# Graph attention loop: value products interleaved bank by bank and two steps behind, densities in halves at pinned places, the entry check at the end of the step

## The chip, the cores and the metric

The kernel runs on one core of one Trainium2 chip. A core has five engines, each with its own in-order instruction queue: TensorE (PE, matrix products into PSUM banks), VectorE (DVE), ScalarE (ACT, functions such as exp and ln), GpSimd (POOL, here mostly the issuer of gathers) and SyncE (SP, issuer of plain transfers). ACT can issue transfers as well. The engines order themselves against each other by semaphores only. The metric is the device time of one execution in microseconds. Before the change the median of three runs is 846.97 us (839.39 to 852.38).

## The reference

A graph of 2708 nodes with 128 features and a 0/1 adjacency matrix `adj` goes through four layers, each `x = x + layer(relu(layernorm(x)))`: an attention layer, a normalised convolution, a convolution with batch norm, and a dense attention layer. The change lies in the last one, but for one line in its preparation:

```python
XW = h @ W
s_col = XW @ a[0, :f]
s_row = XW @ a[0, f:]
Z1 = leaky_relu(s_row[:, None] + s_col[None, :], negative_slope=0.01)
den = exp(Z1)
num = A @ den
att = where(num != 0, den / where(num != 0, num, 1.0), 0.0)
H = A @ (att @ XW)
```

So there are two products with A around a division, and the one in the middle, `att @ XW`, runs over all pairs of nodes.

## The kernel before

`binary` computes everything for a 0/1 matrix and counts entries that are neither 0 nor 1. A `general` path behind it is only entered when that count is above zero.

**Preparation of the last layer (L538 to L1074).** Since `exp(leaky(r + c))` is `exp(r) exp(c)` on one side of a kink and `exp(0.01 r) exp(0.01 c)` on the other, nodes are ranked by their row score, cut into 22 chunks of 124, and columns are grouped by the chunk in which their kink lies. `ranks` (L667) finds the ranks. For each tile t of 128 nodes VectorE compares a row of scores with the tile's own scores (the tile `bits`, t x 128 wide), TensorE adds up its columns (L687), and its row sums go into `rowsum`. For even t VectorE makes the row sums itself, in the same instruction (L680). For odd t VectorE only compares (L674), and ScalarE runs over `bits` again with an accumulating pass (L676). All of `rowsum` is needed for `below` (L789), from which the ranks, the tables of indices and everything after follow. Prefix sums of adjacency rows go to DRAM (`pre_d`, L1070 to L1073).

**The attention loop (L1169 to L1208).** It has NE = 22 steps. Each step covers 128 columns of `den` against all 2708 nodes, in two half steps q = 2s and 2s + 1. What a step needs and makes:

- *Rows.* For each half step a gather `g` fetches 124 rows of the transposed adjacency as 8-bit numbers (`fetch`, L1127), a gather `r` fetches 4 rows of prefix sums straight into the last rows of the moving operand (`fetch_pre`, L1130), and VectorE widens `g` into the first 124 (`widen`, L1138 to L1141). Once a step, a gather `xw` fetches the 128 value rows (`fetch_xw`). All five go through GpSimd (L1079). `g` has 4 buffers, `r` has 4, `xw` has 4.
- *Densities.* `densities` (L1095 to L1121) makes the stationary operands for four half steps at once, every second step: eight exponentials on ScalarE (`z` L1113, `lower` L1114), and on VectorE a maximum (L1115), a rounding (`d_hi`, L1118) and the remainder (`d_lo`, L1119), all 512 wide. The column scores come from a transfer on SyncE (`c_row`, L1110), for the first eight half steps (FIRST = 8) from a TensorE product with `diag` (L1100, L1107). `z` and `lower` have two buffers.
- *Sums.* For each of six banks of up to 512 nodes, four matmuls (L1180: two half steps, high and low part) add up `num` in one of two PSUM buffers, and ScalarE takes its logarithm from there (`ln`, L1182).
- *Weights.* ScalarE takes exp(-ln) over the whole 2708 (L1191) and VectorE multiplies with the numerator into `e` (L1193).
- *Value products.* TensorE adds `xw` times `e` to six accumulator banks. `spread_values(s - 1)` (L1146 to L1152) issues the six products of the step before in one block, after the six banks of sums of this step.
- *Check.* In every even step ScalarE's queue issues a load of one tile of the transposed adjacency (1354 KB, L1206), and in the step after VectorE checks it (`check`, L425 to L429, a pass over 2708 columns).

**What sets the order.** Instructions under `tc.keep_in_program_order` keep their order among each other on their engine. All others are placed by the framework's planner. Pinned are the sum and value matmuls, `ln`, the exponential L1191, `e`, `widen` and the loads for the check. The density work of ScalarE and VectorE, the check itself and the gathers are not pinned. On VectorE the recorded order of a pair of steps in the middle of the loop is: `r`, `r` (widen), `chk`, `r`, `r`, `e`, `d_hi`, `d_lo`, `z`, `e`. In that order the check stands ahead of the widening of a step.

**After the loop.** The last step's weights are made in six pieces, the value products of step 21 are added (L1281) and turned (`values`, L1235), and the last product with A (L401) begins. Its moving operand comes from 8-bit tiles `a8`: group 0 is loaded into the buffer that the checks used (`slot`, one buffer, loaded by ScalarE's queue, L1218), groups 1 to 5 by SyncE (L1229). VectorE and ScalarE widen them (L394, L392).

## Time and profile before

The profiled execution took 844.06 us, of which the trace covers 841.9 us (the span). Busy times in it:

| engine | busy us | share of the span | instructions |
|---|---|---|---|
| PE | 687.0 | 82% | 2700 |
| DVE | 578.8 | 69% | 1063 |
| ACT | 440.7 | 52% | 633 |
| POOL | 261.5 | 31% | 187 |

Places in the span (us from its start), by the timeline:

| from | to | what |
|---|---|---|
| 388 | 430 | ranks of the last layer |
| 493.87 | 754.07 | sums of the attention loop, first matmul of step 0 to last of step 21 |
| 754.07 | 768.83 | value products of steps 20 and 21; wait for the first tiles of the last product |
| 768.83 | 841.9 | last product with A, output |

The loop's steps can be told apart by the start of the wide exponential L1191, one per step (the last step's in pieces): 502.90, 516.40, 527.98, 537.77, 556.06, 566.74, 581.18, 592.96, 605.66, 616.86, 633.35, 644.33, 654.23, 664.10, 673.97, 688.85, 698.83, 709.29, 719.17, 735.13, 745.00, 754.72.

How to read a line of the timeline: start, duration, engine, line of the kernel, operation, output <- inputs with their shapes, the number of instructions merged into the line, and in brackets the idle time before it with what ended that idle time. A line of a group has the count, then busy time and mean ns of one, then the idle time ahead of the group's instructions.

### The profile page before, as it was taken

The page shows a single profiled execution, that of the slowest core. Times are in us where ns is not written, and L with a number is a line of the kernel's source. Part 1 is how long each engine was busy: PE and PEld are TensorE (multiplying, and loading weights), DVE is VectorE, ACT ScalarE, POOL GpSimd, SP SyncE. Part 2 cuts the span into 40 slices and gives each one's busy share as a digit, 9 for nine tenths or more (in the row PEclk, how much of TensorE's full clock was granted, in tenths as well). Part 3 has the DMA queues.
Part 4 walks back from the last instruction along what each step waited for, and adds up shares of the span by engine and source line. Part 5 has one row for each costly group of instructions (what it writes and reads, how often), then busy time and mean ns, then how long its engine had stood idle before and what let it go on. Part 6 is the DMA issues. An engine that isn't in the chain of part 4 may idle for free.

```text
span 841.9 us, 8176 instructions
## 1 busy us (share of the span) xinstructions
PE 687.0 (82%) x2700; PEld 420.6 (50%) x2700; DVE 578.8 (69%) x1063; ACT 440.7 (52%) x633; POOL 261.5 (31%) x187
## 2 busy tenths in 40 slices
PE   3899999918778789968759746978879989897995
PEld 2443343316556557644337334545546656464884
DVE  4886879577976666558999568556668756765433
ACT  3646766550662565348720387664645646462552
POOL 3101112220000010012002266756786888820000
PEclk9999999967999899988979869988999999898998
DMA  9189999801998154201001355654344445418002
GB/s 335 38 319 411 424 402 382 318 18 65 394 408 307 51 182 157 67 7 39 31 1 28 96 134 137 156 123 132 93 106 135 133 127 155 131 50 315 1 13 57
DMA packets 46521, 136.30 MB, mean 162 GB/s; under 512 B 13041, under 2 KB 24803, under 8 KB 38939
## 3 DMA queue, kind: packets, MB, share of 16 engines
q1 hardware_dynamic: 28341, 93.85, 30.6%
q0 software_dynamic: 15840, 25.82, 10.8%
q10 hardware_dynamic: 2289, 16.02, 6.3%
q8 instruction: 23, 0.38, 0.2%
q14 instruction: 28, 0.22, 0.1%
HBM read 116.84 MB, written 18.77 MB: 161 GB/s over the span
## 4 chain that ended last, share of the span: by engine, by line
PE 24%; DVE 12%; DMA 9%; issue 4%; ACT 4%; POOL 2%; DVEq 0%; POOLq 0%; ACTq 0%
PE acc L401 7%; PE bank L1180 7%; PE acc L1149 6%; DMA g<-adjt_d,row_i 4%; DMA chk<-in_adj_t_dram 4%; DVE r L1140 2%; DVE bits L680 2%; PE acc L825 1%; DMA a<-adjt_d 1%; DVE e L1193 1%; ACT ln L1182 1%; POOL r L1079 1%; ACT z L1113 1%; ACT lower L1114 1%; DVE own L659 1%
## 5 line engine op out<-in xcount | busy, mean ns | idle before, releaser
L1180 PE MATMUL bank<-r,d_hi 128*128 128x512 f32 (+1 forms) x264 | 109.6, 419 | 39.7 <-ACT ln L1182 24.2
L1182 ACT ACTIVATE ln<-bank,tiny 128x512 f32<-128x512 f32 x132 | 81.8, 634 | 86.0 <-PE bank L1180 83.0
L1149 PE MATMUL acc<-e,xw 128*128 128x512 f32 x252 | 107.3, 578 | 3.6 <-DVE e L1193 3.6
L1079 POOL DMA_INDIRECT g<-adjt_d,row_i x44 | 89.0, 2022 | 46.9 <-DVE row_i L1006 29.4
L1180 PE MATMUL bank<-r,d_lo 128*128 128x512 f32 (+1 forms) x264 | 101.9, 395 | 0.0
L280 PE MATMUL acc<-tau,hw 128*128 128x512 f32 (+1 forms) x240 | 97.2, 551 | 2.6 <-DVE tau L291 2.1
L392 ACT CAST m<-a 128x2048 fp32r<-128x2048 fp8e4 (+1 forms) x44 | 58.2, 1322 | 65.9 <-PE acc L401 57.8
L1193 DVE SCALAR_TENSOR_TENSOR e<-row_b,sig,ln 128x2708 f32<-128x2708 f32 (+2 forms) x27 | 67.3, 2511 | 34.4 <-ACT ln L1191 34.4
L394 DVE CAST m<-a 128x2048 fp32r<-128x2048 fp8e4 (+2 forms) x59 | 56.1, 954 | 47.0 <-PE acc L401 28.5
L1180 PEld LDWEIGHTS bank<-r,d_hi 128*128 128x128 f32 x264 | 53.3, 202 | 69.2 <-ACT ln L1182 44.2
L291 DVE SCALAR_TENSOR_TENSOR tau<-row_b,sg,a 128x1536 f32<-128x1536 f32 (+1 forms) x44 | 70.4, 1627 | 24.2 <-DMA a<-in_adj_dram 16.3
L1079 POOL DMA_INDIRECT r<-pre_d,pre_i x44 | 74.7, 1698 | 26.5 <-PE bank L1180 11.0
L1140 DVE CAST r<-g 124x2708 fp32r<-124x2708 fp8e4 x44 | 69.3, 1609 | 17.7 <-DMA g<-adjt_d,row_i 11.8
L1149 PEld LDWEIGHTS acc<-e,xw 128*128 128x128 f32 x252 | 49.4, 203 | 58.7 <-issue 54.7
L155 POOL TENSOR_TENSOR rstd<-isq,neg_half 128x4 f32<-128x4 f32 (+1 forms) x24 | 23.3, 972 | 169.2 <-DVE isq L154 155.9
L401 PE MATMUL acc<-m,y_hi 128*128 128x512 f32 (+1 forms) x132 | 54.1, 413 | 25.3 <-DVE m L394 22.6
L309 ACT ACTIVATE a<-a 128x2708 fp8e4<-128x2708 f32 x22 | 54.1, 2457 | 39.2 <-issue 22.4
L280 PEld LDWEIGHTS acc<-tau,hw 128*128 128x128 f32 x240 | 42.5, 190 | 61.5 <-issue 50.5
L401 PE MATMUL acc<-m,h_hi 128*128 128x512 f32 (+1 forms) x132 | 53.0, 406 | 7.4 <-ACT m L392 6.6
L1180 PEld LDWEIGHTS bank<-r,d_lo 128*128 128x128 f32 x264 | 53.7, 203 | 7.2
L1079 POOL DMA_INDIRECT xw<-xw_d,xw_i x22 | 44.5, 2020 | 34.4 <-PE acc L1149 18.0
L1191 ACT ACTIVATE ln<-ln 128x2708 f32<-128x2708 f32 (+2 forms) x27 | 54.6, 2041 | 0.6
(437 smaller groups left out, 1265.0 us busy)
## 6 DMA issues: line engine op xcount, KB each, us to landing
a<-in_adj_t_dram SPq DMA_DIRECT2D x25, 1354.0 KB
a<-in_adj_dram SPq DMA_DIRECT2D x21, 1354.0 KB
chk<-in_adj_t_dram ACTq DMA_DIRECT2D x10, 1354.0 KB
adj_d<-a POOLq DMA_DIRECT2D x22, 338.5 KB
adjt_d<-adjt SPq DMA_DIRECT2D x5, 1354.0 KB
a<-adjt_d SPq DMA_DIRECT2D x4, 1354.0 KB
a<-adj_d SPq DMA_DIRECT2D x5, 1024.0 KB
c_row<-ctwo_d SPq DMA_DIRECT2D x9, 256.0 KB
```

Of the source, the lines that this page charges most:

```text
L280: nc.tensor.matmul(accs[b][:, : hi - lo], stationary, tau[b // 3][:, o : o + hi - lo], start=first, stop=last)
L291: nc.vector.scalar_tensor_tensor(tau, row_b[:, h0:h1], sg[:, t : t + 1], a[:, h0:h1], ALU.max, ALU.mult)
L392: nc.scalar.copy(m[:, : hi - lo], src[:, lo:hi])
L394: nc.vector.tensor_copy(m[:, : hi - lo], src[:, lo:hi])
L401: nc.tensor.matmul(accs[b][:, : hi - lo], part[:, t, :], m[:, lo - base : hi - base], start=first and i == 0, stop=last and i == 1,)
L1079: return nc.gpsimd.indirect_dma_start(out=out, out_offset=None, in_=src, in_offset=bass.IndirectOffsetOnAxis(ap=idx, axis=0),)
L1140: ins = nc.vector.tensor_copy(rows_r[q][:CH], g[:CH])
L1149: m = nc.tensor.matmul(ys_acc[b][:, : hi - lo], xws[s], e[:, lo:hi], start=(s == 0), stop=(s == NE - 1))
L1180: m = nc.tensor.matmul(num[:, : hi - lo], d, a[:, lo:hi], start=(i == 0), stop=(i == 3))
L1182: tc.keep_in_program_order(nc.scalar.activation(ln[:, lo:hi], num[:, : hi - lo], AF.Ln, bias=tiny))
L1191: tc.keep_in_program_order(nc.scalar.activation(ln[:, lo:hi], ln[:, lo:hi], AF.Exp, scale=-1.0))
L1193: nc.vector.scalar_tensor_tensor(e[:, lo:hi], row_b[:, lo:hi], sig[:, s : s + 1], ln[:, lo:hi], ALU.max, ALU.mult)
```

## The change

The sums, products, gathers and checks stay the same in number and size. These things are different:

- **Value products.** Step s issues the value products of step s - 2, and bank by bank: four sum matmuls of bank b, then the value product of bank b. Those of step 20 come after the loop, those of step 21 where they were. `e` gets 3 buffers (2 before), `xw` gets 5 (4).
- **Densities.** Each step makes those of two half steps, for the step two later. The four exponentials are pinned, two after the logarithm of bank 1 and two after that of bank 2. The three VectorE instructions are 256 wide and are issued before the step's two widenings. `z` and `lower` get 3 buffers of half the width. `c_row` comes in 20 transfers half as wide, fetched two steps ahead. The first densities are four half steps (FIRST = 4), after the first two widenings instead of before.
- **Check.** It is pinned at its place in the program: the end of the step after the load, behind `e`. In the last step this is behind the last piece of `e`.
- **Ranks.** ScalarE makes the row sums of all tiles with t > 5 (of odd t before), VectorE those of t = 1 to 5 (of even t before).

In the recorded order of the changed kernel, VectorE's instructions of a step are: `z`, `d_hi`, `d_lo`, `r`, `r`, `e`, and after every second step `chk`. ScalarE's are: `ln`, `ln`, `z`, `lower`, `ln`, `z`, `lower`, `ln`, `ln`, `ln`, and the wide exponential.

```diff
-            if t % 2:
+            if t > 5:
                 ts_(bits[:r, : t * P], row_b[:r, : t * P], r_of[:r, t : t + 1], None, ALU.is_gt)
...
-    FIRST = 8
+    FIRST = 4
...
+    def exponents(s, p, z, lower, q):
+        nc_s = nc.scalar.activation
+        tc.keep_in_program_order(
+            nc_s(z[:, q, :], p[:, cols(q)], AF.Exp, bias=r_hi[:, s : s + 1], scale=slope_hi)
+        )
+        tc.keep_in_program_order(
+            nc_s(lower[:, q, :], p[:, cols(q)], AF.Exp, bias=r_lo[:, s : s + 1], scale=slope_lo)
+        )
+
+    def density_tiles():
+        z = steps.tile([P, 2, P], F32, tag="z", name="z", bufs=3)
+        lower = steps.tile([P, 2, P], F32, tag="lower", name="lower", bufs=3)
+        return z, lower
+
+    def densities(s0, z, lower):
         nc.vector.tensor_max(z, z, lower)
-        d_hi = steps.tile([P, 4, P], F32R, tag="d_hi", name="d_hi", bufs=4)
-        d_lo = steps.tile([P, 4, P], F32R, tag="d_lo", name="d_lo", bufs=4)
+        d_hi = steps.tile([P, 2, P], F32R, tag="d_hi", name="d_hi", bufs=4)
+        d_lo = steps.tile([P, 2, P], F32R, tag="d_lo", name="d_lo", bufs=4)
         nc.vector.tensor_copy(d_hi, z)
         nc.vector.tensor_sub(d_lo, z, d_hi.bitcast(F32))
...
+    def fetch_c(s0):
+        c_rows[s0] = p = steps.tile([P, 2 * P], F32, tag="c_row", name="c_row", bufs=4)
+        nc.sync.dma_start(p, ctwo_d[s0 * P : (s0 + 2) * P].partition_broadcast(P))
...
-        w = xws[s] = last.tile([P, P], F32, tag="xw", name="xw", bufs=4)
+        w = xws[s] = last.tile([P, P], F32, tag="xw", name="xw", bufs=5)
...
-    def spread_values(s):
-        e = waiting.pop(s)
-        for b, (lo, hi) in enumerate(E0):
...
+    def spread_value(s, b):
+        lo, hi = E0[b]
+        m = nc.tensor.matmul(
+            ys_acc[b][:, : hi - lo], xws[s], waiting[s][:, lo:hi], start=(s == 0), stop=(s == NE - 1)
+        )
+        tc.keep_in_program_order(m)
...
-        if s % 2 == 0 and FIRST + 2 * s < NS:
-            densities(FIRST + 2 * s)
+        coming = FIRST + 2 * s
+        if coming + 4 < NS:
+            fetch_c(coming + 4)
+        if coming < NS:
+            z, lower = density_tiles()
...
             tc.keep_in_program_order(nc.scalar.activation(ln[:, lo:hi], num[:, : hi - lo], AF.Ln, bias=tiny))
+            if coming < NS and 1 <= b <= 2:
+                exponents(coming + b - 1, c_rows[coming], z, lower, b - 1)
+            if s > 1:
+                spread_value(s - 2, b)
+        if coming < NS:
+            densities(coming, z, lower)
...
-        e = last.tile([P, N], F32, tag="e", name="e", bufs=2)
+        e = last.tile([P, N], F32, tag="e", name="e", bufs=3)
...
-        if s:
-            spread_values(s - 1)
         if pending:
-            check(*pending.pop())
+            tc.keep_in_program_order(check(*pending.pop()))
...
+    for b in range(NB):
+        spread_value(NE - 2, b)
```

## The prediction

> **What bounds the kernel now.** I read the chain of waits first. Inside the attention loop it runs over the landing of the check's tile, VectorE, ScalarE's exponentials and the sums, so the loop is not simply full of matmuls. Then I dated the steps by the wide exponential. From step 11 to 14 they are 9.9, 9.87 and 9.87 us apart. This is TensorE's own pace: in the chain of waits such a step is 5.28 us of sums and 4.59 us of value products. Steps 0 to 11 take 141.4 us against 11 x 9.87 = 108.6, so 32.9 are lost. Steps 14 to 19 take 61.2 against 49.4, so 11.8 are lost. The two losses have different causes.
>
> The first, in the timeline of one slow step:
>
> ```profile
> 541.47 2.98 DVE L427 SCALAR_TENSOR_TENSOR chk<-chk 128x2708 f32<-128x2708 f32 x1 [4.99 <-DMA chk<-in_adj_t_dram]
> ...
> 544.37 3.05 DVE L1140 CAST r<-g 124x2708 fp32r<-124x2708 fp8e4 x2
> ...
> 547.34 3.02 DVE L1193 SCALAR_TENSOR_TENSOR e<-row_b,sig,ln 128x2708 f32<-128x2708 f32 x1
> ...
> 550.74 0.69 DVE L1119 TENSOR_TENSOR d_lo<-z,d_hi 128x512 fp32r<-128x512 f32 x1
> 551.46 0.49 ACT L1113 ACTIVATE z<-c_row,r_hi,slope_hi 128x128 f32<-128x128 f32 x1 [7.13 <-DVE d_lo L1119]
> ...
> 552.58 0.79 PE L1180 MATMUL bank<-r,d_hi 128*128 128x512 f32 x1 [7.00 <-ACT ln L1182]
> ```
>
> VectorE stands at the check until its tile has landed. The remainder `d_lo` comes four instructions later, ScalarE needs it to reuse `z`, the logarithms are queued behind that exponential, and TensorE lacks a bank.
>
> The second, by GpSimd's groups in the two parts of the loop (494 to 643, then 643 to 742):
>
> ```profile
> L1079 POOL DMA_INDIRECT g<-adjt_d,row_i x24 | 46.1, 1919 | 11.7 <-issue 6.1 <-DVE r L1140 4.7 <-DVE d_lo L1119 0.6
> L1079 POOL DMA_INDIRECT r<-pre_d,pre_i x22 | 31.4, 1428 | 15.3 <-PE bank L1180 10.4 <-issue 4.6 <-PE acc L1149 0.3
> L1079 POOL DMA_INDIRECT xw<-xw_d,xw_i x10 | 25.6, 2558 | 19.2 <-PE acc L1149 18.0 <-issue 1.2
> ```
>
> ```profile
> L1079 POOL DMA_INDIRECT g<-adjt_d,row_i x16 | 38.0, 2377 | 4.9 <-issue 4.9
> L1079 POOL DMA_INDIRECT r<-pre_d,pre_i x18 | 37.6, 2088 | 5.5 <-issue 4.9 <-PE bank L1180 0.6
> L1079 POOL DMA_INDIRECT xw<-xw_d,xw_i x8 | 13.3, 1664 | 2.4 <-issue 1.8 <-PE bank L1180 0.6
> ```
>
> In the first part GpSimd waits for others (34 us besides its 0.3 us gaps). In the second it waits for nobody: 42 gathers in 99 us, 2.36 us each with the gap, or 11.8 us for the five of a step, more than TensorE's 9.87. Undisturbed ones take 0.88 to 1.3 us. The long ones end just after a VectorE instruction:
>
> ```profile
> 512.88 2.98 POOL L1079 DMA_INDIRECT g<-adjt_d,row_i  x1 [0.30 <-issue]
> ```
>
> A check ran from 511.72 to 514.63; this gather ended at 515.86, 1.23 us later. So GpSimd's pace depends on how densely VectorE works.
>
> **The change part by part.** I call T the start of a step's first sum.
>
> *Alternation.* 24 sum and 12 value matmuls stay, at 9.87 us. A first sum matmul after value products is followed 0.33 us later instead of 0.23. The change makes six such turns a step, where there was one. But the first matmul of nearly every bank already shows 0.33, so I take 0; the upper end is 5 x 0.1 x 20 = 10 us, the lower 0 since no matmul goes. A bank of sums and its values take 0.93 + 0.85 us, so bank 2 needs bank 0's logarithm at T + 3.56. The wide exponential of the step before ends at T + 2.5 and the logarithm (0.63) at T + 3.15: covered.
>
> *Pinned densities, check last.* The chain above goes: with three buffers of `z` and the check behind `e`, no exponential waits for a check. The check's tile took 9 to 13.5 us from issue to use; it now has about 15. What is late next is VectorE itself. The exponentials (0.385 each) follow the logarithm of bank 2, whose sums are complete at T + 4.5, and end at T + 6.0. Three density instructions at half width: from 0.69, 0.43 and 0.69 at 512, I estimate 0.43, 0.29 and 0.43, each after the other, 1.2 us. Then two widenings (1.48 each): T + 8.7 and T + 10.2. The next step begins at T + 9.87 and needs the second row 0.46 later. That just fits. After a check it doesn't: `e` starts when the wide exponential ends (T + 2.5), takes 2.95, the check 2.98, so the densities begin at T + 8.45 and the rows are there at T + 11.1 and 12.6. TensorE loses 12.6 - 10.33 = 2.3 us, in two pieces of 1.3 and 1.0. With 0.3 for the widenings that GpSimd stretches (3.35 for two in place of 3.05) a pair of steps costs 19.74 + 2.6 = 22.3 us. The density work, ahead of TensorE before, is now a link from each step to the next.
>
> *Gathers.* Their number stays. VectorE's work per step is 1.2 + 2.96 + 2.95 + 1.49 = 8.6 us; at 11.15 us a step it is busy 77%, at 11.8 us 73%. In 643 to 742 it was busy some 70%. So the 2.36 us apply, and GpSimd, not VectorE, sets the pace at 11.8. Bounds: 2.14 (the first part's busy time and gaps, 120 us for 56) and 2.5 (11 gathers from 643.33 to 670.97, VectorE at 79%). I take 2.36, the longer stretch.
>
> *First steps.* The first widenings now stand ahead of `diag`, and the second waits for the prefix sums to be written (GpSimd waited for the same until 485.41). Then: widening to 486.7, `diag` 487.4, product 489.5, four exponentials 490.9, densities and first sum at 492 instead of 493.87. Steps 0 and 1 have no values, and step 1 waits for the widening behind the densities. By the durations above T of step 3 comes at about 521 (before: 528).
>
> *Loop end.* By VectorE: 521 + 9 x 22.3 + step 21 = 732. By GpSimd: at step 3, 87 gathers are left (17 steps of five and two), 87 x 2.36 = 205, to 726; 2 us of landing, then step 21: 738. At 2.14 it would be 719, below VectorE's; at 2.5, 751. Before: 754.07. So **-16 us**, from -22 to -3.
>
> The page "SBUF — State Buffer" of the Trainium skill, section "Who interferes with whom", says that two-port copies and casts lock GpSimd out, while a VectorE instruction with two SBUF inputs only holds up GpSimd's reads, and it infers that writing descriptors is not a read. By this the widenings would block and `e` and the check would not. The sum by it: 6.8 us of undisturbed gathers and gaps and 2.96 of widenings a step, below 9.87, so GpSimd would never bind and the loop would end at VectorE's 732. The gather beside the check above took 2.98 us, so I follow the row.
>
> *Ranks.* VectorE's gain is no gain if ScalarE becomes late:
>
> ```profile
> core 0: us, PE busy (x) PEld busy (x) DVE busy (x) ACT busy (x) POOL busy (x), PEclk, DMA share, GB/s
> 394.00:400.00 6.00, 4.85 (x25) 1.97 (x24) 6.00 (x17) 5.89 (x21) 0.00 (x0) 1.00 0.15 48
> 400.00:428.00 28.00, 20.71 (x96) 8.79 (x94) 27.53 (x69) 20.02 (x49) 1.29 (x1) 0.94 0.07 23
> ```
>
> VectorE is full here, and ScalarE works 25.9 of 34 us. The passes for t = 6, 8, ... 20, between their odd neighbours (0.79 at 640 columns, 2.44 at 2688), add 0.9 + 1.1 + 1.3 + 1.5 + 1.7 + 1.9 + 2.1 + 2.3 = 12.8; t = 5 saves 0.8. That is 38 us of work in 34. Less a microsecond from t = 1 and 3, the last row sum comes 3 us later than 427.6, and `below` with all behind it too. VectorE's saving of some 6 us is idle time. Taken: **+3** (from 0, if the planner fills better, to +6, with waits between).
>
> *End.* The check of the last tile (2.96 us, whatever its 20 rows) now stands behind the last `e`, about 5 us after the last sum. Group 0 of `a8` needs its buffer, so that load starts some 7 us later:
>
> ```profile
> 754.92 0.45 ACTq L1218 DMA_DIRECT2D a<-adjt_d  x1
> ...
> 767.21 1.23 DVE L394 CAST m<-a 128x2048 fp32r<-128x2048 fp8e4 x1 [5.35 <-DMA a<-adjt_d]
> ```
>
> It took 12.3 us among others at 400 GB/s. Started later, with 2.6 of 5.8 MB already moved, it lands 2 to 6 us later. Against that, VectorE's recorded order now has the first blocks of `f_hi` and `f_lo` ahead of the widening that waits; before, it stood idle 5.35 us with them behind. From landing to full pace at 780.8 were 13.6 us holding 27 matmuls (6.3 us), so up to 7 can be saved. Taken 0, from -3 to +5.
>
> **Sum**: -16 + 3 + 0 = -13; 844.06 - 13 is about **830** (the own time is 2.9 below the median shown).
>
> **Rivals.** *Gathers keep up* (2.14 or less): the loop ends at 732, -22 + 3, so 825. For it speaks that GpSimd had 34 us of waits in the first part; against it, that it fell behind at 9.87 us a step with VectorE at 79%. *TensorE's pace*: if the widenings are in time in spite of checks, 20 steps of 9.87 after 508 end at 706, giving 799. Against it is the order on VectorE. *Slower, by the clock:* after 1.84 us of idle time (505.98) matmuls stay 0.23 apart, after 2.29 (603.06) they go to 0.43, and step parts after such gaps took 1.8 to 2.9 us more (577.70: 8.8 for 5.9). My gaps of 1.3 and 1.0 are just below; if late gathers join them into one above 2.29, each costs some 2.3. Six such spells eat the gain, 14 make 862. Against it: a step that waits for gathers has that time to spare. *The ends cost more* (ranks +6, end +5, turns +10 in part): 840.
>
> The page "TensorE: Matmul & The Clock Gate", section "What's actually happening", puts the fall to half clock after an idle window of about 3.4 us; by it my gaps would be safe and this rival gone. The row at 603.06 shows it after 2.29, so I keep the rival.
>
> **Chances.** Forecast 0.45, gathers keep up 0.25, TensorE's pace 0.06, the clock 0.12, the ends 0.12. Two per cent, about what a measurement of this kernel tells from no change, is 17 us: 827 and 861. Faster: all of TensorE's pace, most of the second, a fifth of the forecast: 0.38. Slower: most of the clock case: 0.11. Within: 0.51. The range goes from 812 (forecast with all good ends) to 850 (all bad ends and a few cold spells).
>
> **What would show it.** Right: no wait of `z` for `d_lo`; steps of about 11.8 us; gathers back to back with 0.3 us gaps; `e` never waited for by TensorE; last row sum after 430; VectorE ahead of ScalarE in the ranks. Wrong: GpSimd waiting while steps take 9.9; sums waiting over 2.3 us and a clock below 0.9; a landing of the first `a8` later than 14 us after the last sum with TensorE idle.

## The result, and the profile after

The changed kernel takes 845.61 us (median of 20 runs, 841.47 to 849.99), the kernel before 846.6 (20 runs, 838.63 to 853.34). The ratio is 1.0003 with a 95% interval from 0.998 to 1.0026: no difference that can be measured, where 830 was forecast. The ratio compares the means of the runs in the faster of two states that the chip shows, so it is not the quotient of the two medians. The profiled execution took 845.37 us, with a span of 843.6.

Cut at the same events, the two profiles compare as follows. A step starts with its first sum matmul, and "last sum" is the start of the last one.

| stretch | before | after | change | forecast |
|---|---|---|---|---|
| up to the first comparison of the ranks | 388.12 | 386.09 | -2.03 | 0 |
| ranks, first comparison to `below` (L790) | 40.59 | 43.32 | +2.73 | +3 |
| `below` to first sum | 65.16 | 65.09 | -0.07 | -1.9 |
| first to last sum | 260.09 | 253.64 | -6.45 | -14.2 |
| last sum to the end | 87.9 | 95.4 | +7.5 | 0 |

Nothing changed ahead of the ranks. In the profiles shown here they start between 386.09 and 396.50 us, so the first row is chance, and later comparisons are made by stretch. The loop gained less than half of what was forecast, and the end lost about as much as the loop had gained.

In the loop the stall for the check's tile is gone: no exponential waits for `d_lo`. What is there instead is regular. From step 8 on, the steps take 11.56 and 12.21 us in turn, 23.8 a pair (before: 24.05 a pair on the average of steps 6 to 19, by stalls of 4 to 6.5 us in some steps). The timeline of one pair, as start, duration, engine, line, operation, and in brackets the idle time and what ended it:

```profile
682.80 3.04 DVE L1219 SCALAR_TENSOR_TENSOR e<-row_b,sig,ln 128x2708 f32<-128x2708 f32 x1 [1.86 <-ACT ln L1217]
...
685.76 2.98 DVE L427 SCALAR_TENSOR_TENSOR chk<-chk 128x2708 f32<-128x2708 f32 x1
...
688.66 0.42 DVE L1110 TENSOR_TENSOR z<-z,lower 128x256 f32<-128x256 f32 x1
...
689.78 3.04 DVE L1157 CAST r<-g 124x2708 fp32r<-124x2708 fp8e4 x2
...
691.45 0.47 PE L1200 MATMUL bank<-r,d_hi 128*128 128x512 f32 x1 [1.01 <-ACT ln L1202]
...
692.88 0.50 PE L1200 MATMUL bank<-r,d_hi 128*128 128x512 f32 x1 [0.73 <-DVE r L1157]
...
695.71 0.63 PE L1200 MATMUL bank<-r,d_lo 128*128 128x512 f32 x1
...
696.13 0.63 PE L1200 MATMUL bank<-r,d_hi 128*128 128x512 f32 x1
```

The weights wait for the wide exponential, the check follows them, and the densities and the two widenings stand behind the check. So the first row of the next step comes at about 691.3 and the second at 692.8, while TensorE was done at 690.4. It waits 1.0 us and then 0.73 us. (The profile puts the first wait down to a logarithm, but that had ended at 690.56.) After these two short gaps its matmuls stand 0.42 us apart (695.71, 696.13) in place of 0.23. Two windows, one for each step of the pair, with busy time of PE, PEld, DVE, ACT and POOL, then the granted clock, show where this falls:

```profile
679.89:691.45 11.56, 10.16 (x39) 6.35 (x38) 9.63 (x9) 8.95 (x13) 10.34 (x5) 1.00 0.32 82
691.45:703.66 12.21, 11.48 (x37) 7.09 (x37) 7.68 (x7) 6.58 (x10) 10.49 (x6) 0.86 0.63 177
```

The step that begins late runs at 0.86 of the clock, the other at 1.00. A step without any wait would be 9.93 us: five banks of 1.78 from one first matmul to the next (552.82, 554.60, 556.38) and a small one of 1.03. Six turns between sums and values a step therefore cost nothing that shows against the 9.87 of before.

GpSimd's groups from 584.82 to 727.43, as count, busy time and mean ns, and idle time before them with its reasons, look just as the forecast had them:

```profile
L1079 POOL DMA_INDIRECT r<-pre_d,pre_i x24 | 48.2, 2009 | 7.3 <-issue 6.4 <-PE bank L1200 0.9
L1079 POOL DMA_INDIRECT g<-adjt_d,row_i x24 | 46.9, 1956 | 8.7 <-issue 7.0 <-DVE r L1157 1.7
L1079 POOL DMA_INDIRECT xw<-xw_d,xw_i x12 | 26.1, 2172 | 3.7 <-issue 1.8 <-PE bank L1200 1.5 <-PE acc L1165 0.3
```

60 gathers in 142.6 us are 2.38 us each, most of their idle time is the 0.3 us between two of them, and five make 11.9 us. Whether this sets the pace or only keeps up with it can't be told from these lines.

In the ranks the busy engine has changed sides (windows, same columns):

```profile
392.00:398.00 6.00, 5.15 (x24) 1.86 (x22) 5.80 (x16) 5.79 (x21) 0.00 (x0) 1.00 0.16 47
398.00:428.70 30.70, 21.23 (x100) 9.40 (x98) 22.78 (x68) 30.32 (x61) 0.00 (x0) 0.92 0.07 22
```

ScalarE works 36.1 of 36.7 us, VectorE 28.6; before, VectorE was the full one. At the end, again by the timeline:

```profile
752.99 2.96 DVE L427 SCALAR_TENSOR_TENSOR chk<-chk 20x2708 f32<-20x2708 f32 x1
...
755.99 0.39 ACTq L1239 DMA_DIRECT2D a<-adjt_d  x1
...
767.83 1.23 DVE L394 CAST m<-a 128x2048 fp32r<-128x2048 fp8e4 x1 [6.63 <-DMA a<-adjt_d]
...
769.11 0.79 PE L401 MATMUL acc<-m,f_hi 128*128 128x512 f32 x1 [7.54 <-DVE m L394]
```

The last sum came 5.8 us earlier than before (748.14 against 753.96), but the load of group 0 went out 1.07 us later (755.99 against 754.92), since its buffer is held by the last check, and that check now stands behind the last weights. It landed at 767.83 (before: 767.21), and TensorE stood 7.54 us for it.

Not all of the 7.5 us at the end comes from this. Behind the issue of the last output (835.04 before, 835.16 after) nothing is computed any more; from there to the end of the span it took 6.83 us before and 8.42 after. Nothing tried in this study changes that stretch, and it took from 6.1 to 8.8 us in its profiles, so the difference of 1.6 us is taken for chance. From the last sum to that issue the end is 5.9 us longer (87.0 for 81.1).

### The profile page after: what moved, and what is told of

Same layout as the page of the kernel before. It is cut to its first block, busy times and chain, and to the rows that moved or that the text cites. A ratio compares the mean times of both kernels' runs of the same rounds, so it can differ in the third digit from the quotient of the medians.

```text
span 843.6 us, 8224 instructions
## 1 busy us (share of the span) xinstructions
PE 687.0 (81%) x2698; PEld 423.9 (50%) x2698; DVE 579.1 (69%) x1090; ACT 454.0 (54%) x643; POOL 268.0 (32%) x187
## 4 chain that ended last, share of the span: by engine, by line
PE 25%; DVE 15%; ACT 6%; DMA 5%; issue 4%; POOL 2%; DVEq 0%; POOLq 0%; ACTq 0%
PE bank L1200 8%; PE acc L401 8%; PE acc L1165 6%; DVE r L1157 4%; DVE e L1219 2%; DVE chk L427 2%; DMA r<-pre_d,pre_i 2%; ACT ln L1217 2%; PE acc L825 1%; ACT junk L676 1%; DMA a<-adjt_d 1%; DMA g<-adjt_d,row_i 1%; POOL r L1079 1%; DMA pre_d<-pre_lo 1%; ACT ln L1202 1%
## 5 line engine op out<-in xcount | busy, mean ns | idle before, releaser
L1200 PE MATMUL bank<-r,d_hi 128*128 128x512 f32 (+1 forms) x264 | 150.2, 573 | 35.1 <-DMA r<-pre_d,pre_i 13.0
L1202 ACT ACTIVATE ln<-bank,tiny 128x512 f32<-128x512 f32 x132 | 83.7, 635 | 95.4 <-PE bank L1200 92.3
L1165 PE MATMUL acc<-e,xw 128*128 128x512 f32 (+1 forms) x264 | 128.0, 573 | 0.0
L1079 POOL DMA_INDIRECT r<-pre_d,pre_i x44 | 87.9, 1997 | 26.3 <-PE bank L1200 15.0
L1079 POOL DMA_INDIRECT g<-adjt_d,row_i x44 | 82.8, 1883 | 40.5 <-DVE row_i L1006 26.0
L401 PE MATMUL acc<-m,f_hi 128*128 128x512 f32 (+1 forms) x132 | 50.8, 391 | 8.7 <-DVE m L394 8.3
L1165 PEld LDWEIGHTS acc<-e,xw 128*128 128x128 f32 x264 | 50.0, 198 | 12.5 <-issue 2.9
```

Source lines behind the costliest of these rows:

```text
L401: nc.tensor.matmul(accs[b][:, : hi - lo], part[:, t, :], m[:, lo - base : hi - base], start=first and i == 0, stop=last and i == 1,)
L1079: return nc.gpsimd.indirect_dma_start(out=out, out_offset=None, in_=src, in_offset=bass.IndirectOffsetOnAxis(ap=idx, axis=0),)
L1165: m = nc.tensor.matmul(ys_acc[b][:, : hi - lo], xws[s], waiting[s][:, lo:hi], start=(s == 0), stop=(s == NE - 1))
L1200: m = nc.tensor.matmul(num[:, : hi - lo], d, a[:, lo:hi], start=(i == 0), stop=(i == 3))
L1202: tc.keep_in_program_order(nc.scalar.activation(ln[:, lo:hi], num[:, : hi - lo], AF.Ln, bias=tiny))
```

## The experiments

One table for all of them; times by the profile of each, in us. "Pair" is the mean over steps 6 to 19, "loop" is first to last sum, "end" is last sum to end. Ratios are against runs of the kernel before on the same chip; a single run has none.

| kernel | ranks | pair | loop | end | time | ratio (95%) |
|---|---|---|---|---|---|---|
| before | 40.6 | 24.05 | 260.1 | 87.9 | 846.6 | 1 |
| changed | 43.3 | 23.80 | 253.6 | 95.4 | 845.6 | 1.0003 (0.998 to 1.0026) |
| e1 last check first | 43.4 | 23.47 | 249.4 | 91.2 | 841.8 | 0.9973 (0.9931 to 1.0015) |
| e2 no checks | 44.2 | 20.83 | 227.2 | 88.0 | 817.0 | |
| e3 check behind rows | 43.4 | 22.52 | 246.1 | 89.8 | 838.9 | 0.9927 (0.9894 to 0.996) |
| e4 four gathers | 43.2 | 23.54 | 252.1 | 93.7 | 844.7 | |
| e5 e3 with four gathers | 43.5 | 21.12 | 237.5 | 89.0 | 825.0 | |
| e6 half checks | 42.9 | 25.29 | 269.9 | 89.4 | 862.1 | 1.0197 (1.0158 to 1.0236) |
| e7 values in a block | 43.4 | 23.42 | 247.2 | 96.6 | 839.7 | 0.9935 (0.9907 to 0.9963) |
| e8 e7 and e1 | 42.9 | 23.19 | 243.3 | 91.3 | 836.6 | 0.9879 (0.9823 to 0.9935) |
| e9 checks, one load | 43.4 | 23.41 | 249.1 | 93.7 | 847.3 | |
| e10 e7, checks, one load | 43.5 | 22.04 | 237.5 | 95.3 | 833.9 | |
| e11 e8, ranks, pinned turns | 41.6 | 22.41 | 241.6 | 92.6 | 835.3 | 0.9888 (0.985 to 0.9925) |
| e12 e11, values ahead | 40.8 | 23.16 | 245.1 | 92.5 | 836.0 | 0.9841 (0.9759 to 0.9923) |
| e13 filled gap | 42.9 | 23.78 | 253.5 | 94.4 | 848.8 | 1.0044 (1.0012 to 1.0077) |
| e14 block one behind | 40.7 | 22.56 | 243.3 | 91.2 | 830.8 | 0.9831 (0.9761 to 0.99) |
| e15 filled late gap | 43.5 | 22.54 | 248.1 | 95.1 | 843.4 | 0.9978 (0.994 to 1.0015) |
| e16 filled both gaps | 43.5 | 22.62 | 245.9 | 94.7 | 841.3 | 0.9967 (0.9938 to 0.9997) |
| e17 e14, pinned turns | 40.6 | 22.94 | 244.4 | 87.4 | 824.6 | 0.9755 (0.9696 to 0.9815) |

### What sets the pace of the loop: check, gathers or transfers

**e2, no checks:**

```diff
-    unchecked = [t for t in range(T) if t not in done1]
+    unchecked = []
```

> The changed kernel without the eleven checks of the attention loop and their loads (left out: the test of these eleven tiles for entries other than 0 and 1). Theory that VectorE and the clock behind its lateness set the pace: pairs of steps take 23.75 us in the changed kernel, 10.2 in the step without and 13.5 in the step with a check. Without checks all steps take about 10.2 us, the last sum comes some 30 to 33 us earlier (about 716), and group 0 has its buffer at once, so the time falls by 33 to 40, to about 808. The forecast's theory, that GpSimd's gathers set the pace (five a step at 2.36 us with the gap): steps stay at 11.8 us, or go to 10.7 at the 2.14 us of the kernel before where VectorE is less busy; the last sum comes 0 to 20 us earlier, and widenings wait for gathers.

All steps take 10.3 or 10.5 us, the loop is 26.5 us shorter. The forecast's theory allowed 20 at most; VectorE's theory had asked for 30. The clock is 1.00 from 600 to 700 (windows):

```profile
600.00:700.00 100.00, 94.74 (x347) 60.04 (x346) 71.95 (x60) 73.77 (x104) 85.11 (x49) 1.00 0.38 91
```

This takes VectorE's pass, its tile's transfer and some of GpSimd's blocking away at once, so the next two separate them.

**e4, four gathers a step:**

```diff
-        gather(w, xw_d[:, :], xw_i[:, s : s + 1])
+        tc.keep_in_program_order(nc.sync.dma_start(w, xw_d[s * P : (s + 1) * P, :]))
```

> The changed kernel, but the 128 value rows of a step come by a plain transfer on SyncE's queue instead of a gather (left out: the order of these rows, so the values are those of other nodes). GpSimd issues four gathers a step instead of five. The gathers' theory: 4 x 2.36 = 9.4 us a step, so VectorE sets the pace at my 22.3 us for a pair, in place of 23.75: the loop is 10 to 15 us shorter. VectorE's theory: pairs stay at 23.75, the time stays within 3 us of the changed kernel's 845.6.

The steps are 11.6 and 12.2 us in turn, as in the changed kernel to a tenth, from step 8 on. GpSimd now has time, and what it waits for is VectorE (waits of GpSimd, 584 to 728; line, releaser, total us, times, longest):

```profile
POOL g L1079 <- DVE r L1157: 17.1, 5, 4.1
```

So in the changed kernel the gathers follow the pace and don't set it. Their remarkable fit to 11.9 us is that of a queue that is just able to keep up.

**e9, checks with one load:** all passes of the check run over the first tile.

```diff
-            a = slot.tile([P, N], F32, tag="slot", name="chk")
-            tc.keep_in_program_order(
-                nc.scalar.dma_start(a[: rows(t), :], adj_t[t * P : t * P + rows(t), :])
-            )
+            if s == 0:
+                one = slot.tile([P, N], F32, tag="slot", name="chk")
+            a = one
+            if s == 0:
+                tc.keep_in_program_order(
+                    nc.scalar.dma_start(a[: rows(t), :], adj_t[t * P : t * P + rows(t), :])
+                )
```

> The changed kernel with all eleven passes of the check on VectorE, but only the first of their tiles is loaded and all passes run over it (left out: ten tiles and their test). Theory that in the changed kernel the check costs by its time on VectorE and the slow clock behind it, not by its transfer: pairs of steps stay at 23.7 us and first to last sum at 250 to 254. Rival, that the transfer makes the gathered rows late: pairs go to 20.5 to 21.5, first to last sum below 240.

Steps 4 to 16 are 11.6 and 12.2 us in turn (one 12.5), only the last two pairs are shorter; the loop is 249.1, a little below the range that the theory gave and far above the rival's 240. In the changed kernel the check costs mostly by its pass on VectorE: without the transfer the pair is 0.4 us shorter, and late steps still take 12.2 us.

### The slow clock

**e13, e15 and e16, filled gaps.** Three more matmuls between the sums of the first and the second row, into the bank that the next sums overwrite (`ahead` is that bank, taken early). e13 has them in even steps, e15 in odd ones, and e16 has in odd steps also two value-shaped matmuls ahead of the first sum.

```diff
+                if b == 0 and i == 2 and s > 3 and s % 2 == 1:
+                    for _ in range(3):
+                        m = nc.tensor.matmul(
+                            ahead[:, :512], dense[2 * s][0], rows_r[2 * s][:, :512], start=True, stop=True
+                        )
+                        tc.keep_in_program_order(m)
```

> The changed kernel with three more matmuls in every second step (those that begin behind a check, from step 4 on), between the sums of the first and the second row of bank 0, into the bank that the next sums overwrite: 0.7 us of work where TensorE waited 0.73 us for the second row. The check, its place and its lateness stay. Theory that the two gaps (1.0 and 0.73 us) bring the slow clock, and that it costs 1.8 us a pair: the granted clock stays at 1.00, pairs go from 23.8 to about 22, first to last sum from 253.6 to about 237, the time falls by 14 to 18 us. Rival, that VectorE's order sets the pair and the slow clock only fills time that would be waited anyway: pairs stay at 23.5 or more. Rival, that the first gap alone brings it: no change, or 0.7 us longer.

e13 was misplaced: the check that is issued in an odd step runs during the even step after it and delays the rows of the next odd step, so the filled steps were not the late ones. Pairs stayed at 23.78, with 0.7 us more of matmuls in each. So the step that is not late has time to spare: the next one begins when VectorE has its rows ready.

> The changed kernel with three more matmuls (0.7 us, into a bank that the next sums overwrite) in every odd step from step 5 on, between the sums of the first and of the second row of bank 0, where TensorE waited 0.73 us. The step that begins late is the odd one: the check of step s - 2 runs behind the weights, during step s - 1, and delays the rows of step s. Theory that the slow clock costs what it seems to: the clock stays at 1.00, the late step goes from 12.21 to about 10.4, the pair from 23.8 to 22, first to last sum from 253.6 to about 239, the time falls by 13 to 15 us. Rival, VectorE's order alone sets the pair: unchanged within 0.3 us a pair. Rival, the first gap of 1.0 us alone brings the slow clock: the late step stays at 12.2 or grows by up to 0.7.

> The run above, and in the same steps two more value-shaped matmuls (0.9 us) ahead of the first sum, into the bank that this sum overwrites, where TensorE waited 1.0 us. If either gap alone brings the slow clock, this one has pairs of 22 and the run above has not; if both are needed, both have; if the clock has no part in the pair's length, neither has.

With more matmuls in the gap of the late step the clock stays up, by the windows of a pair in e15:

```profile
667.57:678.66 11.09, 10.74 (x40) 6.88 (x40) 8.19 (x7) 7.21 (x11) 9.57 (x6) 1.00 0.65 183
678.66:690.09 11.43, 10.12 (x38) 6.32 (x37) 10.09 (x9) 8.24 (x13) 9.90 (x6) 1.00 0.32 100
```

and the pair goes from 23.80 to 22.54, in e16 to 22.62: more matmuls, a shorter loop. So VectorE's order alone does not set the pair: the slow clock has a part in it. In e15 the first gap is shorter too, 0.4 to 0.8 us, and 0.35 us of the second is left. A lone gap of 1.04 us in it (ahead of 702.75) left the clock at 1.00, which speaks against the rival that the first gap alone brings the slow clock; the second alone was not tried. The gain is 1.25 us a pair and not the expected 1.8, probably since VectorE is next: by the prediction's sum its order needs 22.3. The loop of e15 is 248.1 us, not the expected 239, since the gain of a pair is smaller and since its step 3 took 15.5 us (11.8 in the changed kernel); the time, 843.4, does not differ from the kernel before by more than noise.

### The alternation

**e7, values in a block,** still two steps behind, after the six banks of sums:

```diff
-            if s > 1:
-                spread_value(s - 2, b)
+        if s > 1:
+            for b in range(NB):
+                spread_value(s - 2, b)
```

> The changed kernel with the alternation alone undone: the value products of step s - 2 follow the six banks of sums of step s in one block. Theory that the alternation makes VectorE late, since it moves the wide exponential, the weights and the check behind it from the middle of a step to its end: in a block the sums end at T + 5.3, the weights at T + 11.5, the check at T + 14.4, the rows at T + 17.1 and 18.6, more than a microsecond ahead of T' = T + 19.8. Steps of 10.0 to 10.4 with and without a check, loop 25 to 33 us shorter, time about 815. Rival, GpSimd: 11.2 to 11.8 a step, time 835 to 845. Rival, that the alternation is what helps: ScalarE's exponentials hold up the sums in a block, steps as long as now or longer.

The time is 839.7, and the steps are as the theory has them for most of the loop: 10.57 us with and without a check. In such a step the check and the widenings are over at 669.18, and the next first sum starts at 669.42 without a wait (timeline):

```profile
662.12 2.97 DVE L427 SCALAR_TENSOR_TENSOR chk<-chk 128x2708 f32<-128x2708 f32 x1
...
666.14 3.04 DVE L1157 CAST r<-g 124x2708 fp32r<-124x2708 fp8e4 x2
```

But six steps take 12.4 to 16.1 us. In the longest (timeline):

```profile
610.63 2.08 POOL L1079 DMA_INDIRECT r<-pre_d,pre_i  x1 [0.30 <-PE bank L1200]
...
611.66 0.33 ACTq L1231 DMA_DIRECT2D chk<-in_adj_t_dram  x1
...
613.02 0.88 POOL L1079 DMA_INDIRECT r<-pre_d,pre_i  x1 [0.31 <-issue]
...
621.04 0.76 PE L1200 MATMUL bank<-r,d_hi 128*128 128x512 f32 x1 [5.26 <-DMA r<-pre_d,pre_i]
...
623.65 0.77 PE L1200 MATMUL bank<-r,d_hi 128*128 128x512 f32 x1 [1.41 <-DMA r<-pre_d,pre_i]
```

The two gathers of prefix sums for this step started at 610.63 and 613.02, beside the load of a check's tile, and TensorE had them more than 10 us later. The alternation is thus not free in its order, though it is on TensorE: it stretches the sums over the whole step, so the wide exponential, the weights and the check come when VectorE should widen. In the block the sums end in the middle of the step.

**e10, e7 with one load,** the edit of e9 in e7.

> The same edit in the kernel with the values in a block. There most steps took 10.6 us, and four took 14.2, 19.9, 12.9 and 15.0, with TensorE waiting for rows of prefix sums to land while a check's tile was in transfer. Theory that the transfer beside the gathers makes these four: all steps 10.6, first to last sum 228 to 232 in place of 247. Rival, that GpSimd falls behind by itself: at least half of the 19 us remain.

The steps of 14 and 16 us are gone, and several of 11.3 to 12.2 are left: 237.5, about halfway. The landings show what the transfer does: in e7's loop rows of prefix sums take up to 13.9 us from the start of their gather to their landing (median 6.2), in e10 up to 7.8 (median 5.3), and TensorE waits 4.7 us for them instead of 14.1. So the transfer makes the long stalls. What makes the steps that are left is not shown; GpSimd is busy with few pauses there too. Without the transfers the alternation stands by itself: the loop takes 249.1 us with it (e9) and 237.5 without (e10).

### Other places for the check

**e3, check behind the rows** and ahead of the weights; SyncE loads the tiles (`fetch_check`), and group 0 is issued as in e1.

```diff
+        if s % 2:
+            tc.keep_in_program_order(check(*pending.pop()))
+            if unchecked:
+                fetch_check()
...
         e = last.tile([P, N], F32, tag="e", name="e", bufs=3)
```

> The changed kernel with all its work, but the check stands behind the two widenings of its step and ahead of the weights instead of behind the weights, SyncE's queue instead of ScalarE's loads its tile (as soon as the check before it is done), and group 0 for the last product is issued behind the last logarithm. Theory that VectorE's order sets the pace: the rows end at T + 10.2 (T: start of a step's first sum), the check at T + 13.2, the weights wait 0.8 us for it and end at T + 16.1, the next rows at T + 18.8 and 20.3, where they are needed at T + 19.9 and 20.3: steps of about 10.2 us with and without a check, loop 30 us shorter, end 5 to 7 us shorter, about 810. The gathers' theory: VectorE is busy 84% at that pace, gathers take 2.36 us or more, steps stay at 11.8: loop unchanged, about 839.

VectorE is nearly in time now (TensorE waits for its rows at most 1.0 us at once, 9.2 us in the loop), but the pair only goes to 22.52. TensorE also waits 13.1 us for rows of prefix sums (timeline):

```profile
614.99 3.23 POOL L1079 DMA_INDIRECT r<-pre_d,pre_i  x1 [0.30 <-issue]
...
617.49 0.33 SPq L1188 DMA_DIRECT2D chk<-in_adj_t_dram  x1
...
626.34 0.76 PE L1209 MATMUL bank<-r,d_hi 128*128 128x512 f32 x1 [2.29 <-DMA r<-pre_d,pre_i]
```

They were gathered from 614.99, and the load of a tile went out beside them. The load ahead of the loop also delayed the first rows: their first gather (487.36) to first sum was 13.6 us, against 8.3 in the changed kernel.

**e5, e3 with four gathers** (the edit of e4, and the first tile loaded after step 0).

> The kernel with the check behind the rows, with two edits: the first tile for the checks is loaded at the end of step 0 instead of ahead of the loop, and the value rows come by a plain transfer (left out: their order), so GpSimd issues four gathers a step. In the kernel with the check behind the rows the widenings were in time, and the steps were still 11.25 us on average, some 10.3 and some 13 to 14.5, with rows of prefix sums landing late. Theory that GpSimd was the bound there (11 gathers in 25.9 us, 2.35 each, without a wait): four gathers need 9.4, steps go to 10.0 to 10.4, and first to last sum takes 220 to 225 us instead of 246. Rival: the rows land late because the check's tile (1354 KB) is in transfer beside them, whoever issues them; the slow steps stay, one or so in two, 11 us on average.

The pair goes to 21.12 and the step to 10 to 11 us, with the transfers still there. So behind VectorE stands GpSimd, close by: with the check out of the way, taking a fifth of its gathers gives 1.4 us a pair, where in the changed kernel it gave nothing. (Whether it is GpSimd's time or the place of these gathers in its queue of transfers, the run does not tell.) The loop stayed above the expected 225 by its first steps (38.2 us for three). By the Trainium skill ("SBUF — State Buffer", section "Who interferes with whom") a VectorE instruction with two SBUF inputs only holds up GpSimd's reads. The prediction's estimate by that page left GpSimd below 9.87 us a step, where it does not bind; the gain of e5 over e3 speaks against that estimate, and the measurement decides.

**e6, half checks:** one half of a tile in every step, behind the widenings, in two buffers of half the size.

```diff
+        if s:
+            tc.keep_in_program_order(check(*pending.pop(0)))
...
+    unchecked = [(t, h) for t in unchecked for h in range(2)]
```

> The changed kernel with all its work; the check is cut in two halves of 1354 columns, one in each step, behind the widenings and ahead of the weights; the halves are loaded into two buffers of half the size, by ScalarE's queue behind the wide exponential; group 0 for the last product goes into these two buffers and is issued behind the last logarithm. VectorE's theory: per step rows until T + 10.2, half check until T + 11.7, weights from T + 12.4, no lateness and no slow clock, so steps of 9.9 to 10.3, first to last sum 215 to 222 us instead of 253.6, the time about 805. GpSimd's theory: with VectorE busy 85% five gathers need 11.2 to 11.8 us, first to last sum 240 to 250, the time 830 to 838.

Slower than both kernels, 862.1, which no theory had. VectorE is even and in time; a transfer now starts in every step, and TensorE waits for rows of prefix sums (waits of TensorE from 500 to 770; total us, times, longest):

```profile
PE bank L1212 <- DMA r<-pre_d,pre_i: 36.0, 11, 9.9
```

The longest of these stands ahead of the first sum, as in the changed kernel (9.47 us there). In the loop it is 26.1 us in ten waits, against 3.5 us in three in the changed kernel. The rows take 9.4 us (median) from the start of their gather to their landing; in e9, without transfers beside them, 5.9.

### The end

**e1, last check first:** ahead of the last weights, and group 0 issued behind the last logarithm.

```diff
+        if s == NE - 1:
+            tc.keep_in_program_order(check(*pending.pop()))
+            a8 = {0: slot.tile([P, N], F32, tag="slot", name="a8_0").bitcast(F8).rearrange("p (q i) -> p q i", q=4)}
+            tc.keep_in_program_order(
+                nc.scalar.dma_start(a8[0].bitcast(U8), adjt8_d[: 4 * P, :].rearrange("(q p) i -> p q i", p=P))
+            )
         e = last.tile([P, N], F32, tag="e", name="e", bufs=3)
```

> The changed kernel, but the check of the last tile (step 21) stands ahead of the last weights instead of behind them, and the load of group 0 for the last product is issued by ScalarE's queue right behind the last logarithm, ahead of the last exponentials. Theory: the end of the changed kernel is set by the landing of group 0 (issued 755.99, landed 767.83, 11.84 us), because its buffer is free only after the last check (752.99 to 755.96). Then the load goes out at about 748.8, some 7 us earlier, lands at about 760.6, and the time falls by 5 to 7 us, to about 839. Rival: the transfers of that stretch fill the 400 GB/s (7.3 MB from 748.3 to 767.8), so that what group 0 gains the others lose, and the last product waits for another group: 0 to -2 us, 844 to 846.

Group 0 lands 11.5 us after the last sum instead of 19.7, and the end takes 91.2 us instead of 95.4; up to the issue of the last output it is 82.4 instead of 87.0 (before: 81.1). So the place of the check did cost most of the 5.9 us; 4.6 of them came back. The time as a whole, 841.8, is not clear of noise. TensorE now waits for something else (timeline):

```profile
747.61 0.42 ACTq L1219 DMA_DIRECT2D a<-adjt_d  x1
...
758.70 1.90 ACT L392 CAST m<-a 128x2048 fp32r<-128x2048 fp8e4 x1 [7.70 <-DMA a<-adjt_d]
760.51 0.58 ACT L191 COPY yT<-acc 128x512 f32<-128x512 f32 x1
...
761.14 1.12 PE L182 MATMUL bank<-ident,yT 128*128 128x128 f32 x4 [7.07 <-ACT yT L191]
```

The planner has put ScalarE's copy of the first block that is to be turned behind a widening that waits for group 0.

**e8, e7 and e1 together.**

> The kernel with the values in a block, and the last check ahead of the last weights with group 0 loaded right behind the last logarithm (as in the first run of this study, where first the load landed 8.2 us earlier against the last sum, and the end came 4.2 us earlier). Expected: another 3 to 5 us less than the kernel with the values in a block; 0 if the loads of the last product fill the transfer engines in any case.

836.6, 3 us below e7, with intervals that overlap. **e11** adds two edits, and **e12** one more:

```diff
-            if t > 5:
+            if t % 2:
...
+        if b == 3:
+            for t in range(2):
+                ready[t] = rounded(
+                    a8[0][:, t, :], 0, E0[first_p[-1]][1], nc.scalar if t % 2 else nc.vector, True
+                )
```

(`True` pins the widening; the copies and the first three products of `values` are pinned as well.) In e12:

```diff
-        if s + 2 < NE:
-            fetch_xw(s + 2)
+        while len(xws) < min(NE, s + 3 + min(2 * (s + 1), 6)):
+            fetch_xw(len(xws))
...
-        w = xws[s] = last.tile([P, P], F32, tag="xw", name="xw", bufs=5)
+        w = xws[s] = last.tile([P, P], F32, tag="xw", name="xw", bufs=11)
```

> Values in a block, the last check first, and two more edits: the row sums of the ranks are shared out as before the change (odd tiles on ScalarE), and the first blocks of the turned values are pinned ahead of the first two widenings for the last product, on ScalarE and VectorE. Expected against the kernel with the block and the last check first (0.988 of the kernel before): the ranks take 40.6 us in place of 43.3, so -2.7; from the last sum to the end 88 in place of 91.3, since TensorE stood 7 us there for a copy that was queued behind a widening that waited for its tile, so -3. In all about 831.

> The kernel of the run above with 11 buffers for the value rows in place of 5, so that GpSimd gathers up to eight steps ahead of use, six of these gathers in the first three steps, where it has idle time. If GpSimd's small reserve (five gathers at 2.1 to 2.3 us in a step of 10.6) is what turns the check's transfer into a stall of TensorE, some of the four long steps go: 5 to 12 us less. If the landing beside the transfer alone does it: the same.

The ranks went back to 41.6 and 40.8 us, as expected. The end did not move (92.6, 92.5): two steps behind and in a block, the products of steps 19 and 20 both stand behind the last sum, which is the likely reason (e14 and e17 try it). Gathering the value rows ahead brought nothing that shows.

**e14, block one step behind** (with two buffers for `e`, the ranks as before the change, and e1):

```diff
+        if s:
+            for b in range(NB):
+                spread_value(s - 1, b)
```

> The changed kernel with the value products of step s - 1 (not s - 2) in one block behind the sums of step s, two buffers for the weights, the last check ahead of the last weights with group 0 loaded behind the last logarithm, and the row sums of the ranks shared out as before the change. Against the kernel with the block two steps behind and the last check first: after the last sum there is one block of value products less (4.6 us), so last sum to end goes from 91.3 to about 87 to 88; the ranks take 40.6 to 41.6 us in place of 43.3; the loop stays at 242 to 247. In all about 830. If the end stays above 91, it is not the block.

The end stayed at 91.2: one block less, but without the pins of e11 the copy stands behind the waiting widening again. **e17** has both:

> The kernel with the block one step behind, and the first blocks of the turned values pinned ahead of the first two widenings for the last product. If the two things named above each held the end alone, last sum to end goes from 91.2 to 86 to 88 us and the time from 830.8 to about 827. If something else holds it (the sharing of 400 GB/s among the loads), it stays at 91.

```profile
740.82 0.59 ACT L190 COPY yT<-acc 128x512 f32<-128x512 f32 x1 [1.97 <-PE acc L1166]
743.07 0.59 ACT L190 COPY yT<-acc 128x512 f32<-128x512 f32 x1 [1.67 <-PE acc L1166]
747.82 1.90 ACT L391 CAST m<-a 128x2048 fp32r<-128x2048 fp8e4 x1 [4.16 <-DMA a<-adjt_d]
```

In this timeline of ScalarE the copies stand ahead of the widening, and the end takes 87.4 us. So two things hold the end up, and taking one of them away is not enough: 91.3 us with both (e8), 92.6 with the pins alone (e11), 91.2 with the values one step behind alone (e14), 87.4 with neither. The whole kernel takes 824.6 us, ratio 0.9755 (0.9696 to 0.9815): with all its work it is faster than both. Compared with the changed kernel it keeps the pinned densities and, but for the last step, the check behind the weights; it leaves out the alternation, the second step of delay and the new sharing of the ranks, and pins the first turned values.

## Why the prediction was wrong, point by point

The forecast was -13 us against the profiled execution, and by stretches it missed by +16.7: the end 7.5, the loop 9.5 with its start, the ranks -0.3. Of the 9.5, the first sum is 1.8, steps 0 to 2 are 2.6 and steps 3 to 20 are 4.8. Three steps of the working failed: the end taken at 0, the chain to the first sums, and GpSimd as the pace of the loop. Chance ahead of the ranks took 2.0 off again in these two profiles.

- **The stall of before:** read rightly. It is gone, and what came next was VectorE, as said.
- **Alternation taken at 0:** right on TensorE (9.93 against 9.87 us). But the step failed to ask what the alternation does to the engines that wait for the *last* bank. e7 shows the answer: with the block, a step with a check is not late at all, unless its rows of prefix sums land late. Without the transfers the alternation costs 11.6 us of the loop (e9, e10).
- **VectorE's pair of 22.3 us:** right. The gaps were forecast as 1.3 and 1.0 us and were 1.0 and 0.73; with the clock held up a pair is 22.54 (e15).
- **"GpSimd, not VectorE, sets the pace at 11.8":** failed, though its number came true by luck (11.9). Five gathers at 2.36 us fit the trace of the changed kernel, and e4 shows that a gather less changes nothing. The step took a back-to-back queue in the trace of before for a bound in the kernel after. A bound of that kind is real, but lies lower: e3 and e5. What set the pace is VectorE's order with the slow clock on top: nine pairs of 22.3 and 1.25 us make 212 us for steps 3 to 20, and 211.8 were measured.
- **The clock:** the rival's mechanism decided the pair, and the point from which it decides was wrong. It asked for one gap above 2.3 us, from the row at 603.06 of before. Two gaps of 1.0 and 0.73 us with 0.7 us of matmuls between them were enough. The price was 2.3 us a spell in the prediction, 1.25 us a pair by e15. From steps 3 to 20 the loop took 211.8 us where 207 had been forecast. The Trainium skill ("TensorE: Matmul & The Clock Gate", section "What's actually happening") puts the fall after an idle window of about 3.4 us; the gaps of these steps are 1.3 us and less, and the measurement decides.
- **First steps:** the first sum was forecast 1.9 us earlier and came 0.07 earlier against `below`. The step ended the chain at the widenings and densities. These were ready at 489.3, but the rows of prefix sums have to land:

```profile
494.50 0.76 PE L1200 MATMUL bank<-r,d_hi 128*128 128x512 f32 x1 [9.47 <-DMA r<-pre_d,pre_i]
```

  Their first gather began at 486.21, so this landing took 8.3 us; in the kernel before it lay beside the density work. Steps 0 to 2 then took 31.6 us for 29.
- **Ranks, +3:** right, +2.73; the profiles with the old sharing have 41.6, 40.8, 40.7 and 40.6 us, all with the new one 42.9 to 44.2.
- **End taken at 0, from -3 to +5:** failed, +7.5, of which 5.9 up to the issue of the last output. The landing was forecast 2 to 6 us later against the last sum and was 6.4 (19.69 for 13.25); the error is the other term. "Up to 7 can be saved" behind the landing, by blocks of `f_hi` and `f_lo` ahead of the waiting widening, came to 0.5: from the landing to the issue of the last output 67.3 us, 67.8 before. Two blocks of six had their `f_hi` and `f_lo` early, but the product had waited 7.54 us for group 0, and in the 12.4 us after the landing TensorE's granted clock was 0.70 (0.75 in 13.6 us before).

Of the signs of being wrong that were named, the late landing came (19.69 us after the last sum), and a clock below 0.9 came without the long waits that were to bring it. The low end of the range, 812, does not follow from its terms: with every one at its best end (-22, 0, -3) they give 819.

That the loop's gain and the end's loss are so nearly equal is chance; they have different causes, and e17 keeps the one without the other.

One thing is open: the matmuls of the last product stand 0.233 us apart on average in the changed kernel and 0.229 in the kernel before (same clock, 1.00), about 1 us over its 264 with `f_hi` and `f_lo`. The record narrows it down: the spacing is 0.229 or 0.230 in the three profiles with two buffers of `e` and the values one step behind (before, e14, e17) and 0.233 or more in all with three buffers. Why is not shown. The alternation alone on the kernel before was not tried.

## What to carry to other kernels

A queue that works without a pause may set the pace or only follow it; take a part of its work away before you build a sum on it. When work is spread more evenly over one engine, look at who waits for its last piece: here the spread put a 3 us pass where the next step's operands had to be made. And a buffer that is handed on to the next stage ties that stage to the place of its last user, so a reordering inside a loop has to be followed into what comes after.

## What was not expected of the hardware

- Two idle gaps of 1.0 and 0.73 us within 2.5 us brought TensorE's granted clock to 0.86 over the step; 0.7 us of useless matmuls in the second gap, with gaps of 0.4 to 0.8 and 0.35 us left, kept it at 1.00 and made the loop shorter (e15). A rule is not shown: in the kernel before, gaps of 1.84 and 0.95 us within 4.9 us (504.1 to 509.06) left its matmuls 0.23 us apart.
- A gather of four rows of prefix sums took 8.3 us from its start to its use at the head of the loop, where TensorE stood for it and no check's tile was in transfer (486.21 to 494.50), and over 10 beside one (610.63 to 621.04). Loading the tiles in halves, twice as often, raised the loop's waits for such rows from 3.5 to 26.1 us (e6).
